# Layer 0's table moved to the head of the prologue in a four-layer graph network kernel

## The chip, the cores and the metric

One Trainium2 chip; the kernel runs on one of its cores. A core has five engines that run side by side and meet through semaphores: TensorE (PE, matrix products), VectorE (DVE), ScalarE (ACT), GpSimd (POOL) and SyncE (SP). In this kernel SP issues the plain DMAs and GpSimd the gathers. The metric is the device time of one execution in microseconds (us); the time of a kernel is the median of its runs.

## The reference

Four graph layers on 12,500 nodes of 128 features and 212,500 edges, sorted by target (two random directions and a loop at every node). Each layer gets the normalised, rectified rows, and its result is added to x:

```
h = relu(layernorm(x));  x = x + L0(h)     attention over edges, 4 heads
h = relu(layernorm(x));  x = x + L1(h)     weighted sum over edges, product with W1
h = relu(layernorm(x));  x = x + L2(h)     tensor product with edge features, sum over edges
h = relu(layernorm(x));  x = x + L3(h)     mean over edges, two products, batch norm
```

What the change touches is the start of layer 0. There

```
Wh     = h @ W.T                                   12,500 x 128, in 4 heads of 32
attn_e = leaky_relu(a_src . Wh[src] + a_dst . Wh[dst]) + edge_feat @ W_e.T
alpha  = softmax of attn over the edges of one target
out    = sum over the edges of a target of alpha * Wh[src]
```

For each node the kernel needs the row of Wh, its part of the logit as a source (4 numbers), and its part as a target (4 numbers).

## The kernel before

Everything is in one function, `gnn_kernel`. Outside the layer loops a planner of the compiling framework sets the order of instructions on each engine from the written program and the data dependences; inside the layer loops (`tc.manual_schedule()`) the written order holds. Each engine then runs its list strictly in that order, and so does SP with its DMAs. A DMA from SP takes one of eight semaphores in turn, and so waits until the DMA eight before it has landed.

The stretch ahead of layer 0 is written in this order.

*Constants* (lines 169 to 189): identity matrices, index rows, `eps`, mostly GpSimd.

*Edges* (lines 197 to 332). All edge targets (`di`) and sources (`si`) are loaded as 128 partitions x 207 groups x 8 edges of int32, so each contiguous piece has 32 bytes. The targets are copied to `dpad` in DRAM with padding, and three shifted windows of it are loaded (`seq`). VectorE finds for each group of 1024 edges its first target (`base`), the distance of each edge's target from it (`rel`), and checks whether the edge lists are such that the fast path holds (`bad`, `least`, `end`, `worst`, `rough`). `least` and `end` are filled by some sixty memsets. GpSimd takes a maximum over all partitions (`partition_all_reduce`, line 252). `rel` is transposed by TensorE in 13 blocks, each cast by VectorE (`rl`, two buffers) and stored in DRAM (`rel16`, line 332).

*Weights* (lines 337 to 422). W0, W1, Wl, Wr are loaded and transposed; for W0 the vectors `a` are loaded into `ab` by eight small DMAs, and `WE` gets W0 transposed beside W0 times `a`: 128 columns for Wh, 4 for the source's and 4 for the target's part. Then `WeB`, the blocks `TP` of layer 2's weights, and `mixer`, built by many small VectorE instructions.

*The table* (lines 922 to 956). The rows of x go through in 25 batches of four blocks of 128 rows (the last has two). Per batch: load `xt`; on VectorE `bn_stats`, `bn_aggr`, reciprocal and four normalisations (`norm`, lines 436 to 459), with the square root and one Relu over the batch on ScalarE; four transposes on TensorE, copied from PSUM by ScalarE (`hT`); four products with `WE` into PSUM (`pw`); the first 132 columns are copied by ScalarE to `tt`, the last 4 by VectorE to `sd`. `sd` is split into three bfloat16 terms (five small VectorE instructions), `s3`. `tt` is stored to `tab0`, `s3` to `sdt` in DRAM. All tiles have two buffers.

After it `acc`, the accumulator of layer 0, is cleared by VectorE, and the layer's loop over 208 groups begins: GpSimd gathers rows of `tab0` by `si` (`gather`, line 662), eight gathers of 128 rows a group; SP loads `rel16` and `sdt` for each group (lines 986 to 995).

Of the kernel before, what the change touches and what calls it, by code (L numbers as in the profile page):

```python
# [13 lines left out]
F = mybir.dt.float32  # L14
I = mybir.dt.int32
B16 = mybir.dt.bfloat16
AF = mybir.ActivationFunctionType
ALU = mybir.AluOpType
# [3 lines left out]
PSUM = bass.MemoryType.PSUM  # L22
# [3 lines left out]
P = 128  # L26
T = 8
GE = P * T
W = 128
H = 4  # L30
HD = 32
# [9 lines left out]
NBK = 4  # L41
# [7 lines left out]
RW = 2048  # L49
# [43 lines left out]
def gnn_kernel(ctx: ExitStack, tc, x, src, dst, ef16, ef9, ew, W0, We0, a0, lns, lnb, W1, b1,  # L93
               W2, Wl, bl, Wr, gam, bet, out):
    nc = tc.nc
    N, D = x.shape
# [4 lines left out]
    NB = -(-N // P)  # L101
    LR = N - (NB - 1) * P
    AW = -(-max(NB * P, N + 1 + W) // 4) * 4

    W0_ = NB * 56 // 98 // NBK * NBK
    NW = NB - W0_
    G0 = E * W0_ * P // (N * GE) + 2
# [8 lines left out]
    vec, act, pool, pe = nc.vector, nc.scalar, nc.gpsimd, nc.tensor  # L116

    cst = ctx.enter_context(tc.tile_pool(name="cst", bufs=1))
    dram = ctx.enter_context(tc.tile_pool(name="dram", bufs=1, space=DRAM))
# [27 lines left out]
    def store_rows(d, t, b0, nb, width):  # L147
        for b, n, r in rows(b0, nb):
            nc.sync.dma_start(
                d[b * P : b * P + (n - 1) * P + r, :width].rearrange("(j p) d -> p j d", p=r),  # L150
                t[:r, b - b0 : b - b0 + n, :])

    def load_rows(t, d, b0, nb):
        for b, n, r in rows(b0, nb):
            if r < P:
                pool.memset(t[:, b - b0, :], 0.0)
            nc.sync.dma_start(
                t[:r, b - b0 : b - b0 + n, :],
                d[b * P : b * P + (n - 1) * P + r, :].rearrange("(j p) d -> p j d", p=r))
# [5 lines left out]
    def batches(k):  # L165
        return [(b, min(k, NB - b)) for b in range(0, NB, k)]


    ident = cst.tile([P, P], F, name="ident")
# [8 lines left out]
    eps = cst.tile([P, 1], F, name="eps")  # L178
# [15 lines left out]
        return t  # L194


    si = cst.tile([P, NG, T], I, name="si")
    rel = cst.tile([P, NG, T], F, name="rel")
    bi = cst.tile([P, NG], I, name="bi")
# [1 line left out]
    xall = cst.tile([P, NG], I, name="xall")  # L201
    rough = cst.tile([P, 1], I, name="rough")
    relc = cst.tile([P, NW, NT], F, name="relc")
    early = ExitStack()
    tmp = early.enter_context(tc.tile_pool(name="acp", bufs=1))
    wslot = tmp.tile([P, NW, NT], F, name="wslot")
    bir = tmp.tile([P, NG], I, name="bir")
    relx = cst.tile([P, GM, T], F, name="relx")
# [2 lines left out]
    bi3 = cst.tile([P, NG], I, name="bi3")  # L211
    TOT = PADF + NG * GE + P
    NSG = NG // SG
    NK = -(-NB // NBK)

    done = [min(NG - 1, E * min(NBK * P * (k + 1), N) // (N * GE) + 2) for k in range(NK)]
    assert NG % SG == 0
# [2 lines left out]
    with tc.tile_pool(name="ed", bufs=1) as ep:  # L220
# [52 lines left out]
        vec.scalar_tensor_tensor(worst, red[:, 0, NG:], float(W), most, op0=ALU.mult, op1=ALU.max)  # L273

        least = ep.tile([P, NG], F, name="least")
        vec.memset(least, 0.0)
        for k, g in enumerate(done):
            if g + 1 < NG:
                vec.memset(least[:, g + 1 :], float(min(NBK * P * (k + 1), N)))
        vec.memset(least[:, G0:], float(W0_ * P))  # L280
        for k, g in enumerate(done):
            if g + 1 >= G0 and g + 1 < NG:
                vec.memset(least[:, g + 1 :], float(min(NBK * P * (k + 1), N)))
        vec.tensor_tensor(least, base, least, ALU.is_lt)

        end = ep.tile([P, NG], F, name="end")
        vec.memset(end, float(RW - W))
        for k, g in enumerate(done):
            if g + 6 < NG:
                vec.memset(end[:, g + 6 :], float(NBK * P * (k + 1) + RW - W))  # L290
        vec.tensor_tensor(end, base, end, ALU.is_gt)
        vec.tensor_tensor(least, least, end, ALU.max)

# [11 lines left out]
        with tc.tile_pool(name="bgp", bufs=1, space=PSUM) as pp:  # L305
            pun = pp.tile([P, 2, NW], F, name="pun")
            pe.matmul(pun.rearrange("p k w -> p (k w)"), ones, units.rearrange("p k w -> p (k w)"),
                      start=True, stop=True)
# [16 lines left out]
        with tc.tile_pool(name="edp", bufs=2, space=PSUM) as pp:  # L325
            for c in range(0, NG * T, P):
                n = min(P, NG * T - c)
# [6 lines left out]
    ef9f = ef9.rearrange("e f -> (e f)")  # L334


    WE = cst.tile([P, P + 2 * H], F, name="WE")
    W1T = cst.tile([P, P], F, name="W1T")
    WlT = cst.tile([P, P], F, name="WlT")
    WrT = cst.tile([P, P], F, name="WrT")  # L340
    with tc.tile_pool(name="wt", bufs=2) as wp, tc.tile_pool(name="wtp", bufs=2, space=PSUM) as pp:
        for w, to in ((W0, WE[:, :P]), (W1, W1T), (Wl, WlT), (Wr, WrT)):
            wn = wp.tile([P, P], F, name="wn")
            nc.sync.dma_start(wn, w)
            wps = pp.tile([P, P], F, name="wps")
            pe.transpose(wps, wn, ident)
            vec.tensor_copy(to, wps)
            if w is W0:
                ab = wp.tile([P, 2 * H], F, name="ab", bufs=1)
                vec.memset(ab, 0.0)  # L350
                for h in range(H):
                    for s in range(2):
                        nc.sync.dma_start(ab[h * HD : (h + 1) * HD, s * H + h : s * H + h + 1],
                                          a0[h : h + 1, s * HD : (s + 1) * HD].rearrange("o d -> d o"))
                aps = pp.tile([P, 2 * H], F, name="aps", bufs=1)
                pe.matmul(aps, wn, ab, start=True, stop=True)
                vec.tensor_copy(WE[:, P:], aps)
    WeB = cst.tile([P, T * H], F, name="WeB")
    vec.memset(WeB, 0.0)
    for t in range(T):  # L360
# [61 lines left out]
    vec.memset(ones16, 1.0)  # L422

    acc = SimpleNamespace(t=None, ring=RW)
    tab0 = dram.tile([N, P + H], F, name="tab0")
    sdt = dram.tile([AW, 3 * H], B16, name="sdt")
    lgt = dram.tile([TOT, H], F, name="lgt")
    alt = dram.tile([TOT, H], F, name="alt")
    tab3 = dram.tile([N, 3 * P], B16, name="tab3")
# [6 lines left out]
    def norm(sp, t, nb, out, parts=False):  # L436


        st = sp.tile([P, nb, 6], F, name="st")
        mv = sp.tile([P, nb, 2], F, name="mv")  # L440
        for j in range(nb):
            vec.bn_stats(st[:, j, :], t[:, j, :])
        for j in range(nb):
            vec.bn_aggr(mv[:, j, :], st[:, j, :])
        rs = sp.tile([P, nb], F, name="rs")
        act.activation(rs, mv[:, :, 1], AF.Sqrt, bias=eps)
        yield
        vec.reciprocal(rs, rs)
        h = sp.tile([P, nb, D], F, name="h")
        for j in range(nb):  # L450
            vec.tensor_scalar(h[:, j, :], t[:, j, :], mv[:, j, 0:1], rs[:, j : j + 1], op0=ALU.subtract, op1=ALU.mult)
        if out is None:
            yield h
        elif not parts:
            act.activation(out, h, AF.Relu)
        else:
            act.activation(out[:, :, :HD], h[:, :, :HD], AF.Relu)
            act.activation(out[:, :, HD:].rearrange("p j (k u) -> p j k u", k=3),
                           h[:, :, HD:].rearrange("p j (u k) -> p j k u", k=3), AF.Relu)
# [459 lines left out]
            vec.tensor_tensor(rough[:1], rough[:1], w[:1], ALU.max)  # L919


    WN = P + 2 * H
    with tc.tile_pool(name="p0", bufs=2) as sp, tc.tile_pool(name="p0p", bufs=2, space=PSUM) as pp:
        zs = sp.tile([P, 3 * H], B16, name="zs", bufs=1)
        vec.memset(zs, 0.0)
        for r in range(N, AW, P):
            n = min(P, AW - r)
            nc.sync.dma_start(sdt[r : r + n, :], zs[:n, :])
        for b0, nb in batches(4):
            xt = sp.tile([P, nb, D], F, name="xt")  # L930
            load_rows(xt, x, b0, nb)
            h = sp.tile([P, nb, D], F, name="h0")
            for _ in norm(sp, xt, nb, h):
                pass
            pt = pp.tile([P, nb, P], F, name="pt")
            for j in range(nb):
                pe.transpose(pt[:, j, :], h[:, j, :], ident)
            hT = sp.tile([P, nb, P], F, name="hT")
            act.copy(hT, pt)
            pw = pp.tile([P, 2, 512], F, name="pw")  # L940
            pwv = pw[:, :, : 2 * WN].rearrange("p a (c n) -> p a c n", n=WN)
            for j in range(nb):
                pe.matmul(pwv[:, j // 2, j % 2, :], hT[:, j, :], WE, start=True, stop=True)
            tt = sp.tile([P, nb, P + H], F, name="tt")
            sd = sp.tile([P, nb, H], F, name="sd")
            for a in range(0, nb, 2):
                act.copy(tt[:, a : a + 2, :], pwv[:, a // 2, : min(2, nb - a), : P + H])
                vec.tensor_copy(sd[:, a : a + 2, :], pwv[:, a // 2, : min(2, nb - a), P + H :])

            s3 = sp.tile([P, nb, 3, H], B16, name="s3")  # L950
            for k in range(3):
                vec.tensor_copy(s3[:, :, k, :], sd)
                if k < 2:
                    vec.tensor_tensor(sd, sd, s3[:, :, k, :], ALU.subtract)
            store_rows(tab0, tt, b0, nb, P + H)
            store_rows(sdt, s3.rearrange("p j k h -> p j (k h)"), b0, nb, 3 * H)

    acc.t = tmp.tile([P, RW + W], F, name="acc")
    H1 = H + 1
    vec.memset(acc.t, 0.0)  # L960
    with (tc.tile_pool(name="e0", bufs=2) as sp, tc.tile_pool(name="e0p", bufs=2, space=PSUM) as pp,
          tc.tile_pool(name="n0", bufs=2) as ns, tc.tile_pool(name="n0p", bufs=1, space=PSUM) as np_,
          tc.tile_pool(name="so", bufs=1) as ss, tc.tile_pool(name="sop", bufs=1, space=PSUM) as sps):
# [275 lines left out]
    with (tc.tile_pool(name="t1", bufs=1) as tp, tc.tile_pool(name="e1", bufs=3) as sp,  # L1239
# [16 lines left out]
        with tc.manual_schedule():  # L1256
            g = -1
            while g < G0 + 4 or alive or here or there or waiting:
# [11 lines left out]
                if g == 0:  # L1270
                    full = NB - (LR < P)
                    for b in range(0, full, 14):
                        n = min(14, full - b)
# [7 lines left out]
                h = g - 1  # L1281
                if 0 <= h < G0:
                    p = pags[h] = pag[:, h % 2]
                    s, r = S.pop(h), X.pop(h)
# [73 lines left out]
    with (tc.tile_pool(name="e2", bufs=3) as sp, tc.tile_pool(name="e2p", bufs=2, space=PSUM) as pp,  # L1358
# [9 lines left out]
        with tc.manual_schedule():  # L1368
            mixed[0] = mix(0)
            g = -1  # L1370
# [121 lines left out]
    with tc.tile_pool(name="l3", bufs=1) as lp:  # L1492
        acc.t, acc.ring = lp.tile([P, AW], F, name="acc3"), None
        stats = lp.tile([P, NK, 6], F, name="stats")
        with (tc.tile_pool(name="t3", bufs=1) as tp, tc.tile_pool(name="e3", bufs=2) as sp,
# [12 lines left out]
            with tc.manual_schedule():  # L1508
# [5 lines left out]
                while g < G0 + 8 or alive or going or waiting:  # L1514
# [16 lines left out]
                    h = g - 3  # L1531
# [225 lines left out]
```

## Time and profile before

| | |
|---|---|
| median of 3 runs, without profile | 7498.6 us (7488.39 to 7502.39) |
| the profiled execution's own time | 10246.51 us |
| its span in the profile | 10244.7 us |
| TensorE clock granted over the span | 0.721 |
| edges, weights, other set-up | 0 to 100.2 us |
| table of layer 0 | 100.2 to 232.7 us |
| layer 0 begins (first gather) | 232.69 us |
| VectorE busy, 0 to 232 us | 135.28 us |
| TensorE busy, 0 to 232 us | 87.59 us |
| ScalarE busy, 0 to 232 us | 50.55 us |

The profile is one execution, taken with the hardware profiler, and this program runs much longer under it than without. In a line of the order of time the first number is the start in us from the span's start, the second the time that the work took; then the engine, the line of the program, the operation with its output and input tiles, and in brackets how long the engine had been idle and what ended that. SPq is SP's queue; its durations are those of the issue, not of the transfer. In a line of groups the numbers after the bar are busy us in total, mean ns of one, and idle time before them with what ended it.

### The profile page before, as it was taken

The numbers are of one execution on the slowest core, as the hardware profiler recorded it, in microseconds if no ns is written. First come the engines' busy times: TensorE is split into PE (matmuls) and PEld (weight loads), VectorE is DVE, ScalarE is ACT, GpSimd is POOL, SyncE is SP. The second block draws the span as 40 slices with busy tenths as digits, with TensorE's granted clock in tenths as the row PEclk, the third lists the DMA queues.
The fourth block names the chain that finished last, engine by engine and source line by source line (L and its number), as shares of the span: only waits on it lengthen the run. The fifth ranks groups of instructions, "written<-read, shape, count | busy, mean of one in ns | idle before, by whom it ended". The sixth has DMA issues, their size and how long they took to land. (4 is left out here: it accounts for less than half of the span.)

```text
span 10244.7 us, 122470 instructions
## 1 busy us (share of the span) xinstructions
PE 5782.4 (56%) x41651; PEld 4207.5 (41%) x41652; DVE 5285.8 (52%) x10323; ACT 2834.1 (28%) x7693; POOL 5126.7 (50%) x5372
## 2 busy tenths in 40 slices
PE   3245545443333257777764666666666655666666
PEld 2234434443333235555544655565555641111112
DVE  5466666656666323333344666666666652333334
ACT  1122332333333213333331222222222222333333
POOL 0555555555555355555525555555555535555552
PEclk7566666765655678888876777777777776777777
DMA  5233333333323322222211111111111122222223
GB/s 85 62 71 71 72 72 74 73 74 73 76 71 77 74 59 71 70 72 73 70 50 42 47 47 47 47 49 47 47 48 47 47 83 77 77 77 78 75 79 85
DMA packets 741320, 674.77 MB, mean 66 GB/s; under 512 B 341298, under 2 KB 629427, under 8 KB 740660
## 3 DMA queue, kind: packets, MB, share of 16 engines
q0 software_dynamic: 186624, 382.17, 15.4%
q1 hardware_dynamic: 554057, 284.66, 10.8%
q8 instruction: 329, 5.39, 0.2%
q14 instruction: 310, 2.54, 0.1%
HBM read 603.93 MB, written 63.30 MB: 65 GB/s over the span
## 5 line engine op out<-in xcount | busy, mean ns | idle before, releaser
L664 POOL DMA_INDIRECT X<-tab,si x1664 | 1620.0, 974 | 1506.1 <-DVE msg L1083 705.7
L664 POOL DMA_INDIRECT X<-htab,si x1664 | 1572.1, 945 | 1371.8 <-ACT A L1319 868.4
L672 POOL DMA_INDIRECT X<-htab,si x968 | 937.7, 969 | 696.7 <-PE pag L1287 310.2
L672 POOL DMA_INDIRECT X<-tab,si x968 | 919.2, 950 | 614.8 <-PE pg L1545 217.8
L1087 PE MATMUL pag<-oh,msg 128*128 128x128 f32 x3328 | 732.1, 409 | 376.1 <-DVE msg L1083 334.4
L1087 PEld LDWEIGHTS pag<-oh,msg 128*128 128x128 f32 x3328 | 678.6, 311 | 391.4 <-DVE msg L1083 338.8
L1466 ACT CAST xb<-px 128x384 bf16<-128x384 f32 x1050 | 496.0, 479 | 1171.4 <-PE px L1455 475.2
L1309 PE MATMUL py<-mixer,eT 72*128 72x120 f32 x416 | 158.6, 483 | 1124.4 <-ACT eT L1308 997.8
L1344 PE MATMUL pag<-oh,A 128*128 128x128 f32 x3328 | 712.4, 404 | 0.0
L1224 ACT ACTIVATE xs<-px,wslot 128x128 f32<-128x128 f32 x1050 | 372.9, 367 | 1214.9 <-PE px L1212 557.4
L1344 PEld LDWEIGHTS pag<-oh,A 128*128 128x128 f32 x3328 | 698.4, 319 | 0.0
L1287 PE MATMUL pag<-oh,X 128*128 128x128 f32 x1936 | 457.1, 327 | 333.2 <-DVE acc L1280 162.6
L679 DVE TENSOR_TENSOR oh<-iop,rel 128x1024 f32<-128x1024 f32 (+1 forms) x321 | 389.6, 1214 | 494.0 <-remote 215.5
L1007 PE MATMUL pt<-WeB,eT 128*128 128x32 f32 x416 | 120.5, 380 | 927.4 <-ACT eT L1005 613.8
L1545 PE MATMUL pg<-X,oh 128*128 128x384 bf16 x968 | 398.1, 421 | 425.8 <-DVE f L1538 327.3
L1346 ACT COPY R<-pag 128x256 f32<-128x256 f32 x208 | 77.5, 373 | 1967.5 <-remote 1484.9
L1212 PE MATMUL px<-tabS,oha 128*32 128x128 f32 x8652 | 524.4, 318 | 149.4 <-issue 82.0
L1193 PE MATMUL pw<-ohb,xs 128*128 128x128 f32 x2100 | 587.1, 367 | 12.7 <-ACT xs L1224 11.1
L1309 PEld LDWEIGHTS py<-mixer,eT 72*128 72x128 f32 x416 | 101.5, 303 | 1181.3 <-ACT eT L1308 1047.8
L1455 PE MATMUL px<-tabS,oha 128*32 128x384 bf16 x4326 | 455.5, 409 | 191.9 <-issue 134.0
L1354 DVE TENSOR_TENSOR acc<-acc,po 128x128 f32 x208 | 59.8, 288 | 943.4 <-remote 865.6
L1319 ACT ACTIVATE A<-X,ef 128x128 f32<-128x128 f32 x1664 | 509.5, 390 | 12.3 <-DMA X<-htab,si 12.0
(454 smaller groups left out, 12216.4 us busy)
## 6 DMA issues: line engine op xcount, KB each, us to landing
lob<-lo SPq DMA_DIRECT2D x252, 224.0 KB
rb<-rel SPq DMA_DIRECT2D x208, 256.0 KB
X<-tab,si POOLq DMA_INDIRECT x2632
X<-htab,si POOLq DMA_INDIRECT x2632
xtab<-xv SPq DMA_DIRECT2D x72, 256.0 KB
xv<-xtab SPq DMA_DIRECT2D x72, 256.0 KB
lob<-lo SPq DMA_DIRECT2D x84, 160.0 KB
ef<-in_edge_attr_dram SPq DMA_DIRECT2D x51, 256.0 KB
```

Of the source, the lines that this page charges most:

```text
L664: pool.indirect_dma_start(out=t[:, s, :], out_offset=None, in_=table[:, :], in_offset=bass.IndirectOffsetOnAxis(ap=idx[:, s : s + 1], axis=0))
L672: pool.indirect_dma_start(out=ts[-1], out_offset=None, in_=table[:, :], in_offset=bass.IndirectOffsetOnAxis(ap=idx[:, s : s + 1], axis=0))
L679: vec.tensor_tensor(s, iop[:, None, :].to_broadcast([P, T, W]), r[:, :, None].to_broadcast([P, T, W]), ALU.is_equal)
L1087: pe.matmul(pag[:, 0, :], msg[:, t, :], S[:, t, :], start=t == 0, stop=t == T - 1)
L1193: pe.matmul(pw, x, b, start=j == 0, stop=j == NT - 1)
L1212: pe.matmul(px[q * SL : (q + 1) * SL, :], a[:, jj * P + q * SL : jj * P + (q + 1) * SL], tabS[:, blk, :], start=True, stop=True)
L1287: pe.matmul(p, r[t], s[:, t, :], start=t == 0, stop=t == T - 1)
L1319: act.activation(A[:, t, :], X[:, t, :], AF.Copy, scale=e[:, t, 0:1])
L1344: pe.matmul(pag[: TPK[c] * HD, c, :], lhs, S[:, t, :], start=t == 0, stop=t == T - 1)
L1455: pe.matmul(px[q * SL : (q + 1) * SL, :], a[:, jj * P + q * SL : jj * P + (q + 1) * SL], tabS[:, blk, :], start=True, stop=True)
L1466: act.copy(x[:, : 3 * P], px)
L1545: pe.matmul(p, s[:, t, :], r[t], start=t == 0, stop=t == T - 1)
```

## The change

The table is written first, straight after the constants, and the edges and the other weights behind it.

- `tab0`, `sdt` and `WE` are made first. The loads of x for the first eight batches go ahead of everything on SP; `xt` has nine buffers, and the load of batch k+8 is written at the end of batch k. The other tiles of the batch have three buffers instead of two.
- W0 and `ab` are loaded behind the eight loads of x; W1, Wl and Wr stay where the weights were.
- Rows are normalised by ScalarE: VectorE makes `mr` = -mean x rs, and four ScalarE activations per batch give relu(rs x + mr). The four VectorE normalisations and the one Relu over the batch go.
- `pw` is a PSUM tile for two blocks. Both `tt` and the targets' part are copied from it by VectorE; the latter goes to `sdall`, which holds all nodes.
- The split into three bfloat16 terms is made once over `sdall` after the last batch, and `sdt` is stored once (128 x 97 pieces of 24 bytes, and the remainder) instead of per batch.
- The memsets of `least`, `end` and `acc` go from VectorE to GpSimd.

The diff, cut to its core (the removed table loop at line 922 is described above and is what `-` would show there):

```diff
+    for k in range(8):
+        rows0(k)
+    with tc.tile_pool(name="wt0", bufs=1) as wp, tc.tile_pool(name="wtp0", bufs=1, space=PSUM) as pw_:
+        wn = wp.tile([P, P], F, name="wn")
+        nc.sync.dma_start(wn, W0)
...
+        vec.tensor_copy(WE[:, P:], aps)
+    sdall = sp.tile([P, NB, H], F, name="sdall", bufs=1)
+    for k in range(NK):
...
+        rs = sp.tile([P, nb], F, name="rs")
+        act.activation(rs, mv[:, :, 1], AF.Sqrt, bias=eps)
+        vec.reciprocal(rs, rs)
+        mr = sp.tile([P, nb], F, name="mr")
+        vec.scalar_tensor_tensor(mr, mv[:, :, 0], -1.0, rs, op0=ALU.mult, op1=ALU.mult)
+        h = sp.tile([P, nb, D], F, name="h0")
+        for j in range(nb):
+            act.activation(h[:, j, :], xt[:, j, :], AF.Relu, bias=mr[:, j : j + 1], scale=rs[:, j : j + 1])
...
+        act.copy(hT, pt)
+        tt = sp.tile([P, nb, P + H], F, name="tt")
+        for a in range(0, nb, 2):
+            n = min(2, nb - a)
+            pw = pp.tile([P, 2, WN], F, name="pw")
+            for j in range(n):
+                pe.matmul(pw[:, j, :], hT[:, a + j, :], WE, start=True, stop=True)
+            vec.tensor_copy(tt[:, a : a + n, :], pw[:, :n, : P + H])
+            vec.tensor_copy(sdall[:, b0 + a : b0 + a + n, :], pw[:, :n, P + H :])
+        store_rows(tab0, tt, b0, nb, P + H)
+        rows0(k + 8)
+
+    s3 = sp.tile([P, NB, 3, H], B16, name="s3", bufs=1)
+    for k in range(3):
+        vec.tensor_copy(s3[:, :, k, :], sdall)
+        if k < 2:
+            vec.tensor_tensor(sdall, sdall, s3[:, :, k, :], ALU.subtract)
+    store_rows(sdt, s3.rearrange("p j k h -> p j (k h)"), 0, NB, 3 * H)
...
-        vec.memset(least, 0.0)
+        pool.memset(least, 0.0)
...
-        vec.memset(end, float(RW - W))
+        pool.memset(end, float(RW - W))
...
-        for w, to in ((W0, WE[:, :P]), (W1, W1T), (Wl, WlT), (Wr, WrT)):
+        for w, to in ((W1, W1T), (Wl, WlT), (Wr, WrT)):
...
-    with tc.tile_pool(name="p0", bufs=2) as sp, tc.tile_pool(name="p0p", bufs=2, space=PSUM) as pp:
...
-            for _ in norm(sp, xt, nb, h):
...
-                act.copy(tt[:, a : a + 2, :], pwv[:, a // 2, : min(2, nb - a), : P + H])
-                vec.tensor_copy(sd[:, a : a + 2, :], pwv[:, a // 2, : min(2, nb - a), P + H :])
...
-            store_rows(tab0, tt, b0, nb, P + H)
-            store_rows(sdt, s3.rearrange("p j k h -> p j (k h)"), b0, nb, 3 * H)
...
+    pre.close()
     acc.t = tmp.tile([P, RW + W], F, name="acc")
     H1 = H + 1
-    vec.memset(acc.t, 0.0)
+    pool.memset(acc.t, 0.0)
```

## The prediction

> **What bounds the kernel now.** I read the page first, for the span:
>
> ```profile
> span 10244.7 us, 122470 instructions
> ```
>
> The profiled execution took 10246.51 us, the unprofiled runs 7498.6. All sums below are made against the profiled span; how they carry over is settled at the end of the sum.
>
> The change touches only what runs before the first gather of layer 0, so the second view is the order of time in that stretch. It shows where the parts begin, and two issues on SP's queue that take long:
>
> ```profile
> 1.27 15.34 SPq L127 DMA_DIRECT2D si<-in_src_dram  x1
> 16.67 15.59 SPq L135 DMA_DIRECT2D di<-in_dst_dram  x1
> 100.21 0.39 SPq L157 DMA_DIRECT2D xt<-in_x_dram  x1
> 232.69 1.30 POOL L664 DMA_INDIRECT X<-tab,si  x1 [18.98 <-DVE z L967]
> ```
>
> Edges and weights take 0 to 100.2 us, the table 100.2 to 232.7, one after the other. di and si are cut into 26,496 pieces of 32 B each; whatever is issued behind one waits in SP's queue for some 15.5 us. From 232.7 on GpSimd issues one gather after another, so layer 0 starts when the first gather can. In the built order of the changed kernel each engine's sequence from that gather on is the same as before, so the length of this prologue is the whole effect.
>
> Third, one period of the table loop, from matmul to matmul (186.46 to 191.53, 5.07 us), and the matmul at another moment:
>
> ```profile
> 186.46 2.18 PE L943 MATMUL pw<-WE,hT 128*128 128x136 f32 x8 [0.73 <-ACT hT L939]
> 188.72 0.38 ACT L947 COPY tt<-pw 128x264 f32<-128x264 f32 x1 [2.12 <-issue]
> 189.00 0.63 ACT L455 ACTIVATE h<-h 128x512 f32<-128x512 f32 x1
> 189.68 1.12 PE L937 MATMUL pt<-ident,h 128*128 128x128 f32 x4 [1.04 <-ACT h L455]
> 190.89 0.59 ACT L939 COPY hT<-pt 128x512 f32<-128x512 f32 x1 [0.99 <-PE pt L937]
> 191.53 2.18 PE L943 MATMUL pw<-WE,hT 128*128 128x136 f32 x8 [0.73 <-ACT hT L939]
> ...
> 121.05 1.19 PE L943 MATMUL pw<-WE,hT 128*128 128x136 f32 x8 [0.68 <-ACT hT L939]
> ```
>
> The period is a ring of waits between TensorE and ScalarE: matmuls 2.18, copy tt, Relu, transposes, copy hT, matmuls. ScalarE holds the copy tt ahead of the Relu, so the next batch's transposes wait until this batch's matmuls are done. VectorE lies beside it; its groups from 100 to 232 us (count, then busy us and mean ns):
>
> ```profile
> L451 DVE TENSOR_SCALAR h<-xt,mv,rs 128x128 f32<-128x128 f32 x98 | 28.0, 342 | 0.8
> L442 DVE BATCH_NORM_STATS2 st<-xt 128x6 f32<-128x128 f32 x98 | 23.4, 281 | 7.0 <-DMA xt<-in_x_dram 6.9
> L952 DVE CAST s<-sd 128x16 bf16<-128x16 f32 x72 | 11.8, 164 | 1.5
> L444 DVE BATCH_NORM_AGGREGATE mv<-st 128x2 f32<-128x6 f32 x98 | 10.7, 158 | 0.0
> L954 DVE TENSOR_TENSOR sd<-sd,s 128x16 f32<-128x16 f32 x48 | 8.2, 171 | 1.3
> L948 DVE COPY sd<-pw 128x8 f32<-128x8 f32 x49 | 7.8, 159 | 25.3 <-ACT tt L947 25.3
> ```
>
> **The change, part by part.**
>
> *Period of a batch.* VectorE loses the four normalisations (28.0/25 = 1.1 us a batch) and the splitting (20.0/25 = 0.8). It gains the two copies of tt from PSUM and one small product for the bias. The nearest row for a copy is ScalarE's own 0.38; a VectorE copy of 128x128 out of PSUM (line 347) took 0.29, and 128x1664 elements took 1.88, about 1.05 ns an element, so 264 elements cost 0.29 + 136 x 1.05 ns = 0.43. Two make 0.86. Busy time in the loop was 19.98 of 30 us, 3.35 a batch; 3.35 - 1.9 + 0.86 + 0.15 = 2.5. ScalarE: root 0.30, hT 0.59, four Relus with scale and bias at 0.39 at most (row of line 1319, 390 ns): 2.45 at most. TensorE: the built order puts one transpose of the next batch ahead of the matmuls and three behind, so the ring is matmuls 1.98 (start to the next transpose, at 117.33 and 119.31), three transposes 0.8, wait 0.25, copy hT 0.59: 3.6 us.
>
> Here the Trainium skill weighs in (TensorE: Matmul & The Clock Gate, Part 1): the array runs at half clock by default and sustained activity of some 3.4 us releases it. The trace has both prices, 2.18 and 1.19 for the same eight, and shows half clock (granted 0.50 from 130 us on) at a TensorE that was 65% busy. In the new ring it is 3.3/3.6 = 92% busy. By the row at 2.18 the period is 3.6 and 25 batches take 90 us; by the rule it warms, the ring falls below VectorE's 2.5, and they take 65. A warm TensorE would be (1.19 + 0.55)/2.5 = 70% busy again, near the 65% that was granted half, so I take the middle, 3.1.
>
> *Start.* The batches are 256 KB; one landed 2.7 us after its issue (100.21, statistics at 103.26). Eight at the head of SP's queue, then W and eight pieces of a, put the last of these near 13 us, at about 1 us a batch (320 GB/s were reached in the loop). WE is ready at 14.3, the first tt at 17.5. GpSimd's start (first iota 8.3) is earlier.
>
> *di and si moved into the table.* di's buffer lies where W and a were, so it is issued at about 15 and drains until 31. Queued behind it on SP are the first three stores of tt and the loads of x from batch 10 on. tt has three buffers, so VectorE waits at batch 3 for the first store, until about 33, and behind this copy in its order stand all later statistics and reciprocals, for which ScalarE and TensorE wait. That is a stall of about 10 us. Batches 3 to 7 follow by 45.5. si goes out there and drains until 62; the stores of 8 to 10 and the loads from 18 on are behind it. Batch 11, due at 33 + 8 x 3.1 = 58, waits until 64.5. Batches 12 to 23 take 12 x 3.1 = 37, to 101.5.
>
> *Edges behind the table.* Of the edge work, df, the two reductions, bad1, below and units (9.5 us on VectorE) stand in the order before batch 24; half of it fits into VectorE's slack of 0.6 a batch, so +4. The 830 KB of dpad and three windows of 832 KB (used at 44.29, issued from 39.84) delay stores by up to 9 us against three buffers' slack, +2. That makes 108. What is left then, by the rows of before: the five passes over 128x1664 at 1.9 with the splitting, done once over 392 columns (2.3), and small ones: 12; the all-reduce 0.7 beyond that; base to rough and the scaling of TP 8.8; the remaining rl and rel16 loop 10.2 (11.4 for 13 before); three weights 7.7 (80.65 to 90.5 with four and a before); mixer 9.6; to the gather 1. Sum 50.
>
> *One store for the targets' parts.* 25 stores of 12 KB go, hidden before. One store of 12,416 pieces of 24 B comes, with the 13 rel16 stores queued behind it, for which rl's two buffers wait. By si's row, 15.34 us for 26,496 pieces, it takes 7.2. Against the change speaks the Trainium skill (DMA: Bandwidth & Descriptors, Specifications): below 512 B a transfer is a read-modify-write. No run here separates that for writes; the last 6 us of the prologue, half of whose packets are small stores, spent 17 ns a packet on 16 engines, which would make 13.2 us. Nine are covered by the work from base to the third rl. Without the rule's price the stall is about 1 us with landing, with it 7; I take 5.
>
> *Moved memsets.* VectorE sheds some 60 fills (about 10 us) and acc's 1.87. GpSimd does them from 9 us on and is wanted next for the all-reduce near 118; if its fills were five times dearer it would still be in time. The Relu uses the same activation set, so no load of tables is added.
>
> Total: 108 + 50 + 5 = 163 against 232.7, which is 70 us less of 10244.7. For the unprofiled time I have two bounds: the ratio 7498.6/10246.5 applied to it gives 51, one to one gives 70. The chain of waits puts 21% of the span to "another core or an unknown queue", with its longest pieces all later than 5300 us and no such wait in the prologue, so the surplus of the profile is mostly elsewhere. I take 65: 7498.6 - 65 = 7434.
>
> **The rivals.**
>
> *Stalls take the place (saving 15 to 45).* SP's queue is one line: if stores stuck behind di also hold the loads of x past batch 10, and si again, and the three windows of dpad do not fit the slack, each costs up to 10 more, 7454 to 7484. For it: both 15 us issues, and DMA engines busy 90% while di and si drain. Against it: ten batches of x are on chip before di goes.
>
> *More overlap (saving over 90).* TensorE warm throughout (2.6 a batch: 13 us less) and si early enough to be hidden: under 7409. The single warm row speaks for it, the 0.50 of 100 us against.
>
> *No net change.* The table was 132 us and the edges 100 before; VectorE's sum, 135 us busy of 232, leaves room for it only if stalls of some 55 us arise. About 7499.
>
> *Slower.* One mechanism: the single store of 24 B pieces. It costs net time once it takes 70 us more than I allow, about 83 us in all, or 107 ns a piece on each of 16 engines. At 17 ns it is far off; a row of before for such a store alone is missing. At 130 ns a piece the kernel would take about 7515.
>
> **How the numbers follow.** As computed (saving 45 to 90, 7409 to 7454): 0.60. More overlap: 0.10. Stalls: 0.17. No net change: 0.06. Slower: 0.07. The bound of 0.2% is 15 us, about what three runs here can tell from nothing. Faster is the sum of the first three, 0.87. For 8 in 10 the range takes the likeliest whole, half of more overlap and most of the stalls: 7400 to 7478.
>
> **What would show it.** First gather near 163 (155 to 185 keeps the steps). Copies tt on VectorE near 0.43, Relus below 0.4, periods between 2.6 and 3.6. VectorE idle on the landing of a tab0 store once near 20 to 33 and once near 60. The rel16 loop delayed by no more than 7 us behind the sdt store. Wrong if the gap between the first gather and the end is not that of before within 0.5%, if di holds x back, or if the prologue shrinks in the profile and the runs do not follow.

## The result, and the profile after

The changed kernel takes 7447.2 us (median of 4 runs, 7443.1 to 7458.8) against 7498.9 before (4 runs, 7488.4 to 7502.4): a ratio of 0.9929, 95% interval 0.9918 to 0.9941. That is 51.8 us less, where 65 were predicted. Its profiled execution took 7444.27 us, like its other runs:

```profile
span 7442.5 us, 122320 instructions
```

So the section on the time before is wrong in one point: it is not the profiler that makes this program long. The experiments ran on three chips, and on one of them the kernel before takes 10,268 to 10,311 us in every run, at a granted clock near 0.72 instead of 0.81. The profile at 10,246 us and 0.721 fits such a chip, though its chip is not on record. A profile of the kernel before at 7501 us (first experiment) begins layer 0 at 231.55 us, and that is the number to set the new profile against.

The order of time in the new prologue follows.

```profile
17.50 0.40 SPq L127 DMA_DIRECT2D di<-in_dst_dram  x1
20.47 14.52 SPq L149 DMA_DIRECT2D tab<-tt  x3
36.44 0.43 DVE L260 COPY tt<-pw 128x264 f32<-128x264 f32 x1 [9.55 <-DMA tab<-tt]
...
49.70 0.37 SPq L127 DMA_DIRECT2D si<-in_src_dram  x1
50.95 16.70 SPq L149 DMA_DIRECT2D tab<-tt  x3
69.16 0.43 DVE L260 COPY tt<-pw 128x264 f32<-128x264 f32 x1 [10.45 <-DMA tab<-tt]
...
115.94 23.93 SPq L149 DMA_DIRECT2D sdt<-s  x2
140.39 12.93 SPq L410 DMA_DIRECT2D rel<-rl  x13
143.46 0.49 DVE L409 CAST rl<-prl 128x128 bf16<-128x128 f32 x2 [17.91 <-DMA rel<-rl]
...
170.76 1.29 POOL L729 DMA_INDIRECT X<-tab,si  x1 [54.28 <-DVE z L997]
```

The first gather comes at 170.8 instead of 231.6 us. VectorE stands still three times: 9.6 us behind di, 10.5 us behind si, and 17.9 us behind the single store of the targets' parts. The last of them was priced at 5 us.

Between the stalls the loop is fast. Two batches' matmuls on TensorE in the second half of the table, and two groups of the first 116 us:

```profile
84.90 1.19 PE L259 MATMUL pw<-WE,hT 128*128 128x136 f32 x8 [0.29 <-ACT hT L253]
87.09 1.19 PE L259 MATMUL pw<-WE,hT 128*128 128x136 f32 x8 [0.68 <-ACT hT L253]
```

```profile
L248 ACT ACTIVATE h<-xt,mr,rs 128x128 f32<-128x128 f32 x98 | 40.4, 483 | 5.2 <-DVE mr L245 5.1
L260 DVE COPY tt<-pw 128x264 f32<-128x264 f32 x49 | 21.0, 429 | 28.7 <-DMA tab<-tt 20.0 <-PE pw L259 8.5
```

The eight matmuls take 1.19 us and not 2.18, and from one batch to the next it is 2.46 us (75.37 to 92.59 for seven batches, with two reductions of the edge work, 1.85 us each, among them), where it was 5.07. The copy of tt costs the 0.43 us that was worked out. A Relu with scale and bias lasts 0.48 us, but neighbours overlap: 98 of them kept ScalarE busy for 40.4 us, 0.41 each, against a bound of 0.39.

### The profile page after: what moved, and what is told of

Read it like the earlier page. It is cut to its first block, busy times and chain, and to the rows that moved or that the text cites. A ratio compares the mean times of both kernels' runs of the same rounds, so it can differ in the third digit from the quotient of the medians.

```text
span 7442.5 us, 122320 instructions
## 1 busy us (share of the span) xinstructions
PE 5205.4 (70%) x41651; PEld 3796.7 (51%) x41652; DVE 5238.0 (70%) x10117; ACT 2852.7 (38%) x7717; POOL 5155.7 (69%) x5434
## 4 chain that ended last, share of the span: by engine, by line
PE 23%; POOL 16%; issue 11%; DVE 9%; DMA 5%; ACT 1%; DVEq 1%; SPq 0%; POOLq 0%; ACTq 0%
POOL X L729 15%; PE pw L1223 5%; PE px L1242 5%; PE px L1485 3%; PE pw L1471 3%; PE pag L1317 3%; PE pg L1575 2%; DMA X<-htab,si 2%; DMA X<-tab,si 2%; POOL X L737 2%; DVE oh L748 1%; DVE B L1356 1%; DVE part L1359 1%; PE pag L1374 1%; DVE term L1365 1%
## 5 line engine op out<-in xcount | busy, mean ns | idle before, releaser
L1117 PE MATMUL pag<-oh,msg 128*128 128x128 f32 x3328 | 650.1, 375 | 416.0 <-DVE msg L1113 388.0
L1117 PEld LDWEIGHTS pag<-oh,msg 128*128 128x128 f32 x3328 | 600.5, 279 | 432.8 <-DVE msg L1113 395.8
L1374 PE MATMUL pag<-oh,A 128*128 128x128 f32 x3328 | 563.7, 342 | 0.0
L1374 PEld LDWEIGHTS pag<-oh,A 128*128 128x128 f32 x3328 | 545.6, 256 | 0.0
L1223 PE MATMUL pw<-ohb,xs 128*128 128x128 f32 x2100 | 545.1, 344 | 0.0
L1106 ACT ACTIVATE oh<-iop,far 128x128 f32<-128x128 f32 x1664 | 451.6, 383 | 41.4 <-DVE ohj L947 33.3
L1223 PEld LDWEIGHTS pw<-ohb,xs 128*128 128x128 f32 x2100 | 337.0, 202 | 222.3 <-issue 220.8
L1374 PE MATMUL pag<-oh,B 128*128 128x128 f32 x3328 | 439.0, 289 | 0.0
L1317 PEld LDWEIGHTS pag<-oh,X 128*128 128x128 f32 x1936 | 328.8, 213 | 204.6 <-DVE acc L1310 138.3
L1374 PEld LDWEIGHTS pag<-oh,B 128*128 128x128 f32 x3328 | 428.8, 208 | 0.0
```

What stands on the lines that cost most here:

```text
L1106: act.activation(S[:, t, :], iop, AF.Abs, bias=far[:, t : t + 1])
L1117: pe.matmul(pag[:, 0, :], msg[:, t, :], S[:, t, :], start=t == 0, stop=t == T - 1)
L1223: pe.matmul(pw, x, b, start=j == 0, stop=j == NT - 1)
L1317: pe.matmul(p, r[t], s[:, t, :], start=t == 0, stop=t == T - 1)
L1374: pe.matmul(pag[: TPK[c] * HD, c, :], lhs, S[:, t, :], start=t == 0, stop=t == T - 1)
```

## The experiments

My theory: the saving is the faster loop plus the overlap with the edge loads; what is missing against the sum is the 24-byte store, with rel16's stores queued behind it on SP. The main rival: the DMA engines themselves are full while small pieces drain, so that neither another queue nor more buffers help. A first gather can be compared from chip to chip: it came at 230.2 to 232.7 us in three profiles of the kernel before, at either clock. Whole times are compared only on one chip, each as a ratio to the kernel before there.

### The kernel before, profiled again

No edit.

> The kernel before, unchanged, profiled once more, since its one profile took 37% longer than its runs. Theory: in an execution near 7500 us its prologue is shorter than in that profile, the first gather at 220 to 226 us instead of 232.7, so that the 61.9 us of the profiles and the 51.8 us of the runs are the same saving. Rival (the prologue took the same time in both): first gather at 231 to 234, and 10 us of the saving are given back later than the first gather.

It took 7501.2 us, and began layer 0 here:

```profile
231.55 1.29 POOL L664 DMA_INDIRECT X<-tab,si  x1 [19.07 <-DVE z L967]
```

The rival holds: the prologue is as long as in the first profile. Ahead of the first gather 60.8 us are saved, and some 9 of them do not show in the medians. They are taken up again below.

### The new loop in the old place

```diff
-    (table loop ahead of the edges)
...
+    (the same loop, with its eight loads of x, behind edges and weights)
```

> One part alone: the new table loop (ScalarE normalises, VectorE copies tt, eight loads of x ahead, targets' parts split and stored once) stands where the old one stood, behind edges and weights. Theory (the loop and the overlap both count): edges and weights about 95 us, the first batches 5, 24 further periods of 2.5 to 2.8 us 60 to 67, split 2.5 and the store of the targets' parts, now with nothing over it, 24 to 30: first gather at 190 to 205 us of the profile, so 20 to 35 us behind the full change and 30 to 40 ahead of the kernel before; ratio to before 0.995 to 0.997. Rival A (the faster loop does it all, turning round is worth nothing): first gather near 171, ratio 0.993. Rival B (only the overlap counts): near 232, ratio 1.000. This also tells whether the loop alone brings TensorE to its full clock: pw at 1.19 us from some batch on if so, at 2.18 throughout if the early edges' pauses matter.

Measured: 7468.6 us (5 runs), ratio 0.9960 (0.9947 to 0.9974), first gather at 200.62 us. The last 27 us of its prologue, in order of time:

```profile
174.54 21.24 SPq L149 DMA_DIRECT2D sdt<-s  x1
199.67 0.06 DVE L997 MEMSET z<- 128x4 f32 x1 [25.60 <-DMA sdt<-s]
...
200.62 1.29 POOL L670 DMA_INDIRECT X<-tab,si  x1 [51.78 <-DVE z L997]
```

And the busy time of PE, PEld (TensorE's weight loads), DVE, ACT and POOL in nine batches from the middle of its table, with counts, then the granted clock, the DMA share and GB/s:

```profile
121.10:142.49 21.39, 17.12 (x108) 12.98 (x108) 19.53 (x127) 20.85 (x55) 0.00 (x0) 1.00 0.82 221
```

The theory holds. The loop alone takes 31 us off (231.6 to 200.6), turning the prologue round another 30. With no edge loads beside it the loop runs without a stall. Its first three batches have matmuls at 2.18, 2.18 and 1.64 us; from then on they take 1.19 and start 2.38 us apart (121.10 to 142.49 for nine). In these nine ScalarE is 20.85/21.39 = 97% busy and sets the pace, VectorE 91%, TensorE 80%. From the first load of x to the last copy of tt the table takes 70 us (101.58 to 171.60) instead of 125.5 (100.07 to 225.58). But 25.6 us of this are lost to the store, which has nothing left over it, where the kernel before waited 3.9 us.

What in the loop does it was not separated. In the profile of the kernel before at 7501 us the old loop, too, ran at full clock at first, with batches 2.96 and 2.66 us apart. Then TensorE stood idle for 2.62 us, and from there to the end of the table its matmuls took 2.18 us:

```profile
113.16 1.19 PE L943 MATMUL pw<-WE,hT 128*128 128x136 f32 x8 [0.85 <-ACT hT L939]
...
116.12 1.19 PE L943 MATMUL pw<-WE,hT 128*128 128x136 f32 x8 [0.73 <-ACT hT L939]
...
118.78 1.19 PE L943 MATMUL pw<-WE,hT 128*128 128x136 f32 x8 [0.68 <-ACT hT L939]
122.60 1.11 PE L937 MATMUL pt<-ident,h 128*128 128x128 f32 x4 [2.62 <-ACT h L455]
124.44 2.18 PE L943 MATMUL pw<-WE,hT 128*128 128x136 f32 x8 [0.73 <-ACT hT L939]
```

By these two periods, and only as an estimate, some 2.3 of the 2.7 us that a batch gained go with the clock. Whether the old division of work, with eight loads of x ahead, would have kept the clock up was not tried.

### The single store on another queue

```diff
-    store_rows(sdt, s3.rearrange("p j k h -> p j (k h)"), 0, NB, 3 * H)
+    store_rows(sdt, s3.rearrange("p j k h -> p j (k h)"), 0, NB, 3 * H, nc.scalar)
```

> The full change with one edit: the single store of the targets' parts is issued from ScalarE's queue and not from SP's. Theory (the rel16 stores stand behind its issue in SP's queue, and rl's two buffers make VectorE wait): the wait of rl for a rel16 store, 17.9 us after the change, goes to under 3, the first gather comes at 153 to 157 instead of 170.8; 14 to 18 us, ratio to before near 0.9908. Rival (the 12,416 pieces fill the DMA engines themselves, and anything put on another queue is slowed as much): the wait stays above 8 us and the first gather at 162 or later.

Measured: 7450.7 us (5 runs), ratio 0.9930 (0.9917 to 0.9944), first gather at 170.25: no gain in either.

```profile
118.00 24.46 ACTq L149 DMA_DIRECT2D sdt<-s  x2
124.83 28.05 SPq L410 DMA_DIRECT2D rel<-rl  x13
139.63 0.29 DVE L409 CAST rl<-prl 128x128 bf16<-128x128 f32 x1 [12.02 <-DMA rel<-rl]
```

My theory falls. (ACTq is ScalarE's queue.) The rel16 stores now go out at once, at 124.8, and yet the cast waits 12.0 us for the first of them to land, and 21.8 us over ten waits (24.3 in the changed kernel). The place in SP's queue is worth only 2.6 us: the store itself went out 2.1 us later here (118.00 instead of 115.94), and from it to the first gather it is 52.3 us instead of 54.8. For the rest the DMA engines are at work on the small pieces; in the changed kernel the profile has them busy 90% or more from 117.7 to 140 us. That agrees with the Trainium skill (DMA: Bandwidth & Descriptors, Issuing engines are not separate DMA queues): DMAs share the same engines whoever issues them, and another issuer saves only issue time. Here the price was 24.46 us beside 23.93.

### A row of 32 bytes instead of 24

```diff
-    sdt = dram.tile([AW, 3 * H], B16, name="sdt")
+    sdt = dram.tile([AW, 4 * H], B16, name="sdt")
...
-    s3 = sp.tile([P, NB, 3, H], B16, name="s3", bufs=1)
+    s3 = sp.tile([P, NB, 4, H], B16, name="s3", bufs=1)
+    vec.memset(s3[:, :, 3, :], 0.0)
...
-    store_rows(sdt, s3.rearrange("p j k h -> p j (k h)"), 0, NB, 3 * H)
+    store_rows(sdt, s3.rearrange("p j k h -> p j (k h)"), 0, NB, 4 * H)
```

The two readers of the row, not shown, leave out the fourth group.

> The full change with one size changed: a row of the targets' parts has 32 bytes instead of 24 (a fourth group of zeros), in SBUF and in DRAM; the number of pieces, 12,416, stays. Theory (writes of so small a piece cost about 31 ns on each of 16 engines whatever the size): the store takes 22 to 25 us again, first gather within 2 us of 170.8. Rival (it is the odd 24 bytes, which cut across units of 32: 32-byte pieces of di and si took 9.4 ns each): the store takes 7 to 10 us, and the first gather comes at 155 to 159 us.

Measured, on the chip of lower clock: 10212.1 us (5 runs) against 10281.7, ratio 0.9922 (0.9900 to 0.9944), first gather at 156.24.

```profile
116.79 9.41 SPq L149 DMA_DIRECT2D sdt<-s  x2
126.71 12.14 SPq L411 DMA_DIRECT2D rel<-rl  x13
128.99 0.49 DVE L410 CAST rl<-prl 128x128 bf16<-128x128 f32 x2 [2.58 <-DMA rel<-rl]
...
156.24 1.30 POOL L730 DMA_INDIRECT X<-tab,si  x1 [38.90 <-DVE z L998]
```

The rival holds. A third more bytes in as many pieces take 9.4 us instead of 23.9, and the first gather comes 14.5 us earlier. This is more than the scatter: the store of 24-byte pieces took 21.7 to 24.5 us in six profiles, 22.88 of them on this chip (nine buffers for tt, below), that of 32-byte pieces 7.9 to 9.4 in three. The medians alone don't show it, since the ratio of the changed kernel, 0.9929, lies within this one's interval. What the DMA engines did in the two stretches, first the changed kernel's (115.9 to 140 us), then this one's (116.8 to 126.3):

```profile
DMA packets 12605, 0.34 MB, mean 14 GB/s; under 512 B 12528, under 2 KB 12604, under 8 KB 12604
```

```profile
DMA packets 12623, 0.44 MB, mean 46 GB/s; under 512 B 12555, under 2 KB 12622, under 8 KB 12622
```

The packets are as many. Spread over 16 engines the piece of 24 bytes costs 23.93 x 16/12,416 = 30.8 ns and the one of 32 bytes 9.41 x 16/12,416 = 12.1 ns, each with the start of the transfer in it. The rule of the Trainium skill that the prediction weighed (DMA: Bandwidth & Descriptors, Specifications: below 512 B a transfer is a read-modify-write) cannot be the whole of it, since both sizes lie far below its bound. Whether it is the length of 24 or the start at multiples of 24 instead of 32, was not separated.

### Split and store per batch again

```diff
+        sd = sp.tile([P, nb, H], F, name="sd")
...
-            vec.tensor_copy(sdall[:, b0 + a : b0 + a + n, :], pw[:, :n, P + H :])
+            vec.tensor_copy(sd[:, a : a + n, :], pw[:, :n, P + H :])
+        s3 = sp.tile([P, nb, 3, H], B16, name="s3")
...
+        store_rows(sdt, s3.rearrange("p j k h -> p j (k h)"), b0, nb, 3 * H)
```

> One part of the change undone: the targets' parts are split and stored once per batch again, as in the kernel before. Theory (the store once took 24 us in one piece, of which 17.9 were waited for; per batch it is hidden, but the split costs VectorE 20.0/25 = 0.8 us a batch, and VectorE sets the period of 2.45): the wait of rl falls from 17.9 to under 2, the table takes 0.6 to 0.8 a batch more, 15 to 20 us in all, and about 2 us of split go: first gather at 166 to 173 us, against 170.8. Rival (the split per batch fits in VectorE's slack): 152 to 157. Second rival (the small stores hold tt's stores up as well): 176 or later.

Measured: 10236.4 us (6 runs), ratio 0.9951 (0.9934 to 0.9968), first gather at 188.15. VectorE's waits in the first 130 us (us in total, times, longest):

```profile
DVE tt L260 <- DMA tab<-tt: 26.8, 13, 11.3
DVE s L264 <- DMA sdt<-s: 14.6, 6, 10.4
```

The second rival holds: with this part undone the first gather is 17 us later, not earlier. Stores of 24-byte pieces cost in the loop as well: tt now waits 13 times for a tab0 store, not twice (20.0 us), and the split waits for its own stores. In the kernel before, with 5.07 us a batch, they were hidden. So the single store was no mistake for this loop; its 24 bytes were.

### Nine buffers for tt

```diff
-        tt = sp.tile([P, nb, P + H], F, name="tt")
+        tt = sp.tile([P, nb, P + H], F, name="tt", bufs=9)
```

> The full change with one size changed: tt has nine buffers instead of three. Theory (di and si cost the table time only because tt runs out of buffers while its stores stand behind them in SP's queue): nine batches of slack, 9 x 2.45 = 22 us, cover a drain of 15 us; the two idle times of VectorE behind a tab0 store (9.6 and 10.5 us) go, and the first gather comes at 150 to 158 us, ratio to before 0.989 to 0.992. Rival (the loads of x behind di and si, or the DMA engines being full, take the wait over): VectorE waits as long for x instead, first gather at 165 or later.

Measured: 10231.4 us (6 runs), ratio 0.9950 (0.9931 to 0.9969), first gather at 169.36.

```profile
DVE st L238 <- DMA xt<-in_x_dram: 24.4, 5, 11.1
DVE rl L409 <- DMA rel<-rl: 23.9, 10, 17.5
```

The rival holds. No wait for a tab0 store is left, and 24.4 us of waiting for x are there instead (3.7 us before this edit). Nine batches of slack for the stores are worth nothing when the loads behind di and si come as late.

### Edges first, from ScalarE's queue

```diff
-        load_edges(di, dst, 0, NG, N, 1)
-        load_edges(si, src, 0, NG, 0, 1)
+        load_edges(di, dst, 0, NG, N, 1, nc.scalar)
+        load_edges(si, src, 0, NG, 0, 1, nc.scalar)
```

W0 and `ab` get a place of their own, so that di can go out at once.

> The full change with one edit: di and si are issued from ScalarE's queue at the start, and W and a get a place of their own so that di need not wait for it. Theory (stores of tt and loads of x stand behind the issue of di and si in SP's queue): the two idle times of VectorE behind a tab0 store (9.6 and 10.5 us) go; but ScalarE itself is held by its two issues, about 30 us if each takes 15 as on SP, so that its first square root comes near 30 instead of 14 us. Net of both: first gather 165 to 175 us, within 6 us of 170.8. Rival (DMA engines are full while di and si drain, whichever queue holds them): stalls of 8 us or more on stores or loads of x remain, and the first gather comes at 180 or later.

Measured: 7457.9 us (5 runs), ratio 0.9944 (0.9931 to 0.9958), first gather at 180.43, beyond the theory's range and in the rival's. ScalarE's order at the start:

```profile
0.77 0.49 ACTq L127 DMA_DIRECT2D di<-in_dst_dram  x1
26.07 0.38 ACTq L127 DMA_DIRECT2D si<-in_src_dram  x1
26.54 1.28 ACT L242 ACT_TABLE_LOAD   x1 [26.41 <-DMA di<-in_dst_dram]
26.73 14.51 ACTq L135 DMA_DIRECT2D di<-in_dst_dram  x1
...
41.34 2.42 ACT L248 ACTIVATE h<-xt,mr,rs 128x128 f32<-128x128 f32 x6 [12.83 <-issue]
```

Neither stood quite as written. The two stalls in the loop did go: VectorE waits 1.2 us for tab0 stores and 3.9 for x. But di, with the eight loads of x beside it, held ScalarE until 26 us and not 15, and si until 41. Last of all came a, eight small loads on SP's queue beside di and si; TensorE waited for them, and WE with it:

```profile
45.97 0.57 PE L229 MATMUL aps<-ab,wn 128*128 128x8 f32 x2 [30.70 <-DMA ab<-in_L_gnn_a_dram]
```

The first matmuls of the loop came at 48.2. So 30 us at the start took the place of 20 in the loop. The drain of 31 us of small pieces is paid wherever the table is waiting for DMAs.

### In three portions

```diff
+        if k % 9 == 8 or k == NK - 1:
+            ns = b0 + nb - s0
+            s3 = sp.tile([P, ns, 3, H], B16, name="s3")
...
+            store_rows(sdt, s3.rearrange("p j k h -> p j (k h)"), s0, ns, 3 * H)
```

With nine buffers for tt as well.

> The full change with nine buffers for tt and with the targets' parts split and stored in three portions, after batches 9 and 18 and after the last, each of at most 36 of the 98 blocks. Theory (both losses against the sum are of the same kind, stores behind a long DMA with too few buffers): the two stalls of VectorE behind di and si go, 15 to 20 us, and the last portion takes (26/98) x 24 = 6.4 us under the work from base to the third rl, so that the wait of rl goes, another 15 to 18; the first gather comes at 132 to 142 us, ratio to before 0.987 to 0.990. Rival (the two portions in the loop hold the stores of tt, the loads of x and the edges as long as they took at the end): 150 to 160.

Measured: 10212.2 us (5 runs), ratio 0.9938 (0.9917 to 0.9959), first gather at 172.72.

```profile
DVE st L241 <- DMA xt<-in_x_dram: 33.5, 5, 19.9
DVE rl L414 <- DMA rel<-rl: 6.4, 9, 1.4
```

The theory got the end (the wait of rl is 1.4 us at most) and failed in the loop: the two portions, in the queue beside si, hold x back for up to 19.9 us (the first goes out at 66.6, right behind si's drain). The first gather comes later than even the rival said. Against nine buffers alone the waits for x and for dpad's windows grew by 20 us (33.5 and 11.2 instead of 24.4 and 0.6), and those of rl shrank by 17.5: 24-byte pieces cost in the loop what they cost at the end.

### 32 bytes, and 13 buffers for rl

```diff
-                rl = ep.tile([P, P], B16, name="rl", bufs=2)
+                rl = ep.tile([P, P], B16, name="rl", bufs=13)
```

The row of 32 bytes is in it.

> The full change with rows of 32 bytes for the targets' parts, which brought the first gather from 170.8 to 156.2 us, and with 13 buffers for rl instead of two. Theory (VectorE still waits, at 12 casts, 9.0 us in all, for a rel16 store to land, and each wait is on the way to the first gather): the 13 casts follow one another at about 0.5 us, and the first gather comes at 146 to 150 us. Rival (the next link of the chain is late instead: the weights' loads stand behind the rel16 stores on SP's queue and land no earlier): 153 to 157.

Measured: 7415.5 us (4 runs) against 7495.5, ratio 0.9896 (0.9880 to 0.9913), first gather at 149.73. That is 25 us under the changed kernel on the same chip (7440.3, in the last experiment), and the best of this study. The casts no longer wait:

```profile
126.29 6.06 SPq L411 DMA_DIRECT2D rel<-rl  x13
126.44 0.68 DVE L410 CAST rl<-prl 128x128 bf16<-128x128 f32 x2
```

The last of the 13 casts begins at 128.2 us instead of 138.2. Of those 10 us 6.5 arrive at the first gather; the copy of W1's transpose waits 7.2 us where it waited 4.5.

### si at the end

```diff
-        load_edges(si, src, 0, NG, 0, 1)
...
+        vec.tensor_copy(si[:, 0, :1], rough)
+        load_edges(si, src, 0, NG, 0, 1, nc.scalar)
```

On top of the one before.

> As the one before (32 bytes, 13 buffers for rl), and si is loaded from ScalarE's queue once rough is known (near 126 us), so that its 26,496 pieces move from the middle of the table to the last stretch before layer 0. Theory (what costs is that the pieces fill the DMA engines while the table needs them; at the end they lie beside VectorE's small work): the second stall of the table, 10.7 us, goes, si lands near 126 - 10 + 17 = 133, and the first gather comes at 136 to 143 us. Rival (the stall moves: rel16's stores and the weights' loads now share the engines with si and land 10 us later): 147 to 157.

Measured: 7422.3 us (4 runs), ratio 0.9903 (0.9886 to 0.9919), first gather at 150.33, the same as without it.

```profile
115.51 0.43 ACTq L127 DMA_DIRECT2D si<-in_src_dram  x1
134.40 0.33 SPq L423 DMA_DIRECT2D wn<-in_L_gnn_W_dram  x1
...
137.12 0.29 DVE L426 COPY W1T<-wps 128x128 f32<-128x128 f32 x1 [19.51 <-PE wps L425]
```

The rival holds. The table's last copy of tt begins at 90.6 us instead of 105.8 in the changed kernel, and then VectorE waits 19.5 us for W1 behind si and the rel16 stores. The stall was moved once more, and not removed.

### Where the last 9 us are

The changed kernel and the kernel before, unchanged, on the chip of the last two.

> The full change, unchanged, beside the kernel before and two versions built on it, on one chip. The stretch from layer 0's first gather to layer 1's took 2393.5 us before and 2400 to 2402 us in four kernels with the new loop, where the chip's clock was 0.81; so 8 of the 61 us saved ahead of the first gather would be given back. Theory (layer 0 does lose something, whatever its cause): layer 0 is again 5 us or more longer than that of the kernel before in this call (on a chip at clock 0.72, 15 or more). Rival (that was chance, one profile of the kernel before): within 3 us (clock 0.72: within 10), in either direction.

> The kernel before once more, for the length of its layer 0 beside that of the changed kernel of this call; theory and rival as told for that one. First gather at 231 to 233 us in either case.

The changed kernel took 7440.3 us (4 runs), ratio 0.9926 (0.9909 to 0.9942), with its first gather at 169.48; that of the kernel before came at 230.15. So 60.7 us are saved ahead of the gather and 55.1 in the medians. Layer 0, from its first gather to layer 1's, took 2395.3 us before and 2395.5 after: by the expectation, chance. But over all profiles at the clock of 0.81 it is 2393.5 and 2395.3 in the kernel before, and 2395.5 to 2402.4 in seven with the new loop. From the first gather to the end it is 7268.0 and 7268.4 before, 7271.7 and 7274.7 in the changed kernel, and 7261.6 to 7278.5 in the five built on it. A small loss in layer 0 is neither shown nor excluded; the scatter of one execution is as large as the 6 to 9 us in question.

## Why the prediction was right, and where it was off

*What bounds it.* Right: the effect is the length of the prologue. From the first gather on the two kernels agree to 0.1%.

*Period of a batch.* I took 3.1 us, between 3.6 at half clock and 2.6 at full. It was 2.46, and 2.38 in the old place, with matmuls at 1.19 us: the Trainium skill's rule on the clock (TensorE: Matmul & The Clock Gate, Part 1) was the better guide, and my reason for the middle failed. I had set a TensorE that would be 70% busy at full clock beside the 65% of before, which were counted at half clock. At half clock the new loop kept TensorE busier than that: after di's stall for 6.77 of 7.94 us (85%, from 37.06), and the clock rose at 45.5; after si's for 3.19 of 3.22 us (from 69.78), and it rose at about 72.8. That second rise, after 3 us, agrees with the rule's 3.4 us of sustained activity, while 100 us at 65% brought none. At full clock TensorE was 80% busy in the old place, with 1.90 us a batch instead of the 1.74 that I had given it. Where the border lies between 65% and 85% is not shown. Nor does a pause have to be long to lose the clock: in the kernel before 1.75 us of idle TensorE (122.24 to 123.99) were followed by 0.50 from 124.2 on. ScalarE's 2.45 "at most" held (20.85/9 = 2.32) and is what sets the pace; VectorE's 2.5 was too much (19.53/9 = 2.17).

*Start.* Copy of tt at 17.5 predicted, 19.1 found.

*di and si in the table.* Right in kind and place, low in size. The stalls ended at 36.4 and 69.2 where 33 and 64.5 were given; they cost 9.6 and 10.5 us. Batch 11 was due at 58.7, as given (58), but si went out at 49.7 and not at 45.5, so its drain ended later. The shorter period made up for it: the table's last store went out at 106.2, predicted 108. That this came so close is luck, two misses that offset each other.

The explanation was too narrow, though. I wrote of a line in SP's queue and three buffers. More buffers, another queue and another moment each left the loss where it was or moved it, which points to the 16 engines as what is short while pieces of 32 bytes drain.

*Edges behind the table.* The tail from 106.2 to the first gather took 64.6 us where 55 were given with the stall. The stall explains more than all of it: 17.9 us and not 5. Without it the tail was within 4 us of the sum.

*One store for the targets' parts.* This is the step that failed in size. I had two prices, 7.2 us by the row of si (9.3 ns a piece) and 13.2 by the end of the prologue (17 ns), and held that beyond 9 us it would be seen. It took 23.9, or 30.8 ns, outside both: no row of before was a store of 24-byte pieces in such numbers, and the upper end ought to have been wider. The mechanism, rel16 behind it and rl's two buffers waiting, was the one that I named, save that the engines and not the queue are what it shares.

*From the profile to the runs.* I took 65 between 51 by ratio and 70 one to one. Against a profile at 7501 us the first gather is 60.8 us earlier and the medians 51.8; in the second comparison 60.7 and 55.1. The premise, that the profile's surplus of 37% came from profiling, was wrong; the prologue is equally long at both clocks, so one to one was the right way, and the ratio had no meaning for it. That its 51 lies beside the measured 51.8 is chance.

*The rivals.* "Stalls take the place" named the right terms and overstated them, as they were offset by the warm period. "More overlap" had the period right but not the stalls. The slower case needed 107 ns a piece; at 30.8 it stayed far away.

## What to carry to other kernels

When a DMA is cut into thousands of small pieces, price it in ns a piece on all 16 engines and ask what else needs these engines meanwhile; another issuing queue or more buffers only move the wait. Look at the piece's size in bytes before its number: padding 24 bytes to 32 brought the first gather 14.5 us earlier here and cost one memset and two changed readers. And a loop that frees its engines by a factor of two also uncovers everything that its old slowness hid, the small stores first of all.

## What the runs showed of the hardware that I had not expected

- Stores to DRAM in pieces of 24 bytes took 30.8 ns a piece on each of 16 engines (23.93 us for 12,416), in pieces of 32 bytes 12.1 (9.41 us), while loads in pieces of 32 bytes took 9.3 (15.41 us for 26,496, in the profile of the kernel before at 7501 us).
- TensorE at 65% busy stayed at half clock for 100 us (matmuls at 2.18 us in the kernel before). At 99% busy it left it after 3 us (69.78 to 72.8 in the changed kernel).
- Stores from different queues did not pass each other: beside the sdt store on ScalarE's queue the first rel16 store was there only 14.8 us after its issue (124.83, cast released at 139.63).
- The chips differ: the same program took 7,480 to 7,510 us on two of them and 10,268 to 10,311 on a third, at granted clocks of 0.81 and 0.72 over the span. The prologue was nevertheless the same to 1% (230.2 to 232.7 us).
